# Gate/up units of a fused S4 and feed-forward kernel: a hand-written order of seven slots, and a second DMA queue

## The chip, the cores and the metric

The kernel runs on one core of one Trainium2 chip. The core has a matrix engine (TensorE, PE in the profile), VectorE (DVE), ScalarE (ACT), GpSimd (POOL) and SyncE (SP). Each works through its own instructions in the order in which they were put into its stream, and waits at an instruction until what that instruction needs is there. DMAs are issued from a stream too: here mostly from SP, some from ACT and POOL. The metric is the device time of one execution in microseconds (us), the median of several runs.

## What is computed

`x` is 2048 rows of 1024 floats. Each row is normalized; the result goes through a long convolution along the 1024 columns, whose kernel comes from a small state-space model (S4), and through a feed-forward block with 4-bit weights (64 weights share a scale and a zero). Both are added to `x`:

```python
xn = _layernorm(x, axis=-1)
# S4: 64 states -> 1024 frequencies -> kernel K of 1024 taps
y = jnp.fft.irfft(jnp.fft.rfft(u, n=n) * jnp.fft.rfft(K, n=n), n=n)[..., :L]
return y + D[0] * u
# feed-forward, inter = 2752
g = jnp.einsum('bsh,ih->bsi', x, Wg)
u = jnp.einsum('bsh,ih->bsi', x, Wu)
h = jax.nn.silu(g) * u
return jnp.einsum('bsi,hi->bsh', h, Wd)
```

## The kernel before

**Number format.** Operands of the matmuls are split into two fp16 halves, a high and a low one. A product then takes three matmuls (high·high, high·low, low·high): `PASS`. Every split is a copy to fp16 on ACT (a "hi" step) and a subtraction on DVE (a "lo" step).

**Seven products in place of eight.** The large matrix products use the Strassen-Winograd scheme: of a 2 by 2 product seven block products are made, of sums and differences of blocks. The scheme needs seven factors of each operand (`PROD` names which meet).

**Stages.** First come the norm of `x` and the first weights (to about 135 us). Then the gate/up stage makes `h`; then the convolution (from about 878 us) and the product of `h` with the down weights (from about 1004 us) fill the rest. The change is in the gate/up stage.

**A unit.** The 2752 columns of gate and up are cut into pieces `j` of 128, and the 2048 rows into two halves `cp`. `gate_up(j, cp, wf)` (L597) is one unit: seven products P1 to P7, each 4 x 3 = 12 matmuls of 128x512, into four PSUM banks A, B, C and D. Units for `j` = 0 and 1 are made in another way; `j` = 2 to 20 gives 38 units. P1 goes to A and is copied to B by ACT; P6 adds to B, which is copied to D; P7 goes to C and is copied to the tile `hb`; P2 adds to A. P5 adds to D, and DVE adds D to `hb`; P3 then adds to D; P4 adds to C, which is copied to `ha`, to which DVE adds B. Silu of A and of D on ACT, and two DVE multiplications, give `ha` and `hb`, the two halves of `h`. P5, P4 and P3 of a unit are left for the following unit (`pending`, `rest`, L595 to L612).

**Factors of h.** `finish_h` (L673) makes the factors that the down product will need (`s0` to `s6`) and writes them to DRAM (`HF`), 256 KB each, from SP.

**Weight work beside the units.** It has three kinds. (1) `load_w(gi)` (L409) makes half of the gate/up weights of a piece, a "granule": raw 4-bit values and scales are fetched (`load_raw`), unpacked on DVE, the scales prepared by three instructions on POOL (`scale_c`), sixteen 128x64 activations on ACT apply them (`w_scale`, in three parts), four DVE sums make the factors (`w_sums`), then hi and lo into two tiles `nat`, and two DMA transposes from SP bring them into the tile `wf` that the matmuls read (`w_t`). Four `wf` tiles are there, two pieces' worth. (2) `load_wd(u)` (L461), for u = 0 to 9, makes the factors of the down weights. Its scales and zeros come from DRAM (`SZT`) by four DMAs from SP for each half, in `fetch_wd` (L472); then `dequant`, `sums`, and seven hi and lo steps follow, and each factor goes to DRAM from SP. (3) `s4()` (L853) makes the convolution's kernel by some small DVE operations and a few small matmuls, which borrow a PSUM bank. Both (2) and (3) are generators that the loop of L995 moves on by some steps behind each unit; `lag` (L453) makes a generator wait until a given number of units have ended.

**What sets the order.** In this stage the lines only tell what depends on what. The scheduler of the framework, which runs a model of the times at build, picks the order of the instructions on each engine. Only where an `Engine` has its `pin` set (L66 to L85; at the start of the kernel) does an engine's stream keep the order of the program. Tiles come from pools with a fixed number of buffers: the hi and lo tiles `nat` from five, `ha`/`hb` and their sums from four for even and four for odd `j`, A and C (and S4's banks) from four banks, B and D from two each.

```python
995  for j in range(2, NJ):
996      if 3 <= j < NJ - 1:
997          load_w(2 * j + 2, (j - 1, 1))
998          load_w(2 * j + 3, (j - 1, 1))
999      for cp in range(2):
1000         if cp or j > 3:
1001             gate_up(j, cp, wt[j])
1002         for _ in range(4 if j >= WD_FROM else 0):
1003             next(wd_steps, 0)
1004         for _ in range(3 - cp if j >= S4_FROM else 0):
1005             next(s4_steps, 0)
```

Of the kernel before, what the change touches and what calls it, by code (L numbers as in the profile page):

```python
# [24 lines left out]
F16 = mybir.dt.float16  # L25
# [8 lines left out]
P = 128  # L34
# [4 lines left out]
NJ = 21  # L39
# [48 lines left out]
def build(nc, tc, x, xp, raw_d, sz_d, par_d, vct_d, tab_d, csrow_d, out):  # L88
# [3 lines left out]
    with es:  # L92
# [195 lines left out]
        with ea:  # L288
# [95 lines left out]
            def w_scale(gi, part, behind=None):  # L384
                with tc.issue_after(heads[behind].ins) if behind in heads else nullcontext():
                    scale_a(*made[gi], range((0, 5, 11)[part], (5, 11, 16)[part]))
# [66 lines left out]
            def lag(n=1):  # L453

                n += len(tails)
                while len(tails) < n:
                    yield

            rawd, ready_wd = {}, {}

            def load_wd(u):  # L461
# [10 lines left out]
                def fetch_wd(gi):  # L472


                    raw = rawd.pop(gi)
                    w = wtemp("wd", [P, 8, 256], F32, f"w{gi}")
                    for i in range(2):
                        for b in range(2):
                            SP.dma_start(w[64 * b : 64 * b + 64, 4 * i : 4 * i + 4].rearrange("p f c -> p (f c)"),
                                         SZT[gi - G_WD, 1 - i, b].rearrange("c h -> (c h)").partition_broadcast(64))  # L480
                    q = wtemp("raw", [P, 16, 2, 32], I16, f"qn{gi}")
                    low = raw.bitcast(I16).rearrange("p a (b c) -> p a b c", c=2)[:, :, :, 0]
                    V.tensor_scalar(q[:, :, 0, :], low, 4, 15, ALU.logical_shift_right, ALU.bitwise_and)
                    V.tensor_scalar(q[:, :, 1, :], low, 15, None, ALU.bitwise_and)
                    qt = raw.bitcast(I16).rearrange("p a b -> p (a b)").rearrange("p (a b) -> p a b", a=8)
                    SP.dma_start_transpose(qt, q.rearrange("p a b c -> p (a b c)"))
                    return w, qt

                def dequant(w, qt):
                    x4 = w[:, 0:4]  # L490
                    tt(x4, qt.rearrange("p (f a) b -> p f (a b)", f=4), x4, sub)
                    tt(x4, x4, w[:, 4:8], ALU.mult)
# [16 lines left out]
                if u == 0:  # L509
                    load(ga)  # L510
                    load(gb)
                    yield from lag()
                    ready_wd[ga] = fetch_wd(ga)
                    yield
                ready_wd[gb] = fetch_wd(gb)
                yield from lag(2 if u == 0 else 1)
                ma = ready_wd.pop(ga)
                with tc.issue_after(tails[-1].ins):
                    dequant(*ma)
# [5 lines left out]
                if nxt:  # L525
                    load(nxt[0])
# [4 lines left out]
                lo(5, wa[:, :, 0])  # L531
                mb = ready_wd.pop(gb)
                dequant(*mb)
                wb = blocks(mb[0][:, 0:7])
                yield
                sums(mb[0], True)
                hi(3, wb[:, :, 1])
                tt(wa[:, :, 1], wb[:, :, 1], wa[:, :, 1], sub)
                yield
                if nxt:  # L540
                    load(nxt[1])
                lo(3, wb[:, :, 1])
                hi(7, wa[:, :, 1])
                tt(wb[:, :, 1], wb[:, :, 1], wa[:, :, 0], sub)
                yield

                lo(7, wa[:, :, 1])
                hi(6, wb[:, :, 1])
                if nxt:
                    ready_wd[nxt[0]] = fetch_wd(nxt[0])  # L550
                yield
                hi(2, wb[:, :, 0])
                lo(6, wb[:, :, 1])
# [5 lines left out]
                lo(4, wb[:, :, 0])  # L559
                yield  # L560
# [34 lines left out]
            pending = []  # L595

            def gate_up(j, cp, wf):  # L597
# [12 lines left out]
                def rest(i):  # L610
                    if len(pending) > i:
                        pending[i]()  # L612

                nm = f"{j}_{cp}"
                isc = 1.0 / (XS * WS)
                add, mult = ALU.add, ALU.mult
                bA, bB = bank("A" + nm), bank("B" + nm, "B")
                prod(1, bA, True, True)
                heads[j, cp] = A.copy(bB, bA)
                rest(0)  # L620
                bC = bank("C" + nm)
                prod(7, bC, True, True)
                tag = "h" if j % 2 else "e"
                hb = htile("hb_" + nm, tag)
                A.copy(hb, bC)
                rest(1)
                prod(6, bB, False, True)
                bD = bank("D" + nm, "D")
                A.copy(bD, bB)
                prod(2, bA, False, True)  # L630
                A.activation(bA, bA, AF.Silu, scale=isc)
                rest(2)

                def fifth():
                    prod(5, bD, False, True)
                    tails.append(V.tensor_tensor(hb, bD, hb, add))

                def fourth():
                    prod(4, bC, False, True)
                    ha = htile("ha_" + nm, tag)  # L640
                    A.copy(ha, bC)
                    V.tensor_tensor(ha, bB, ha, add)
                    V.scalar_tensor_tensor(ha, ha, HS * isc, bA, mult, mult)
                    pending[2] = lambda: third(ha)

                def third(ha):
                    prod(3, bD, False, True)
                    A.activation(bD, bD, AF.Silu, scale=isc)
                    V.scalar_tensor_tensor(hb, hb, HS * isc, bD, mult, mult)
                    finish_h(j, cp, ha, hb)  # L650

                pending[:] = [fifth, fourth, None]

            def settle():
                for i in range(len(pending)):
                    pending[i]()
                pending.clear()
# [15 lines left out]
            def finish_h(j, cp, ha, hb):  # L673
                nm = f"{j}_{cp}"
                if j == NJ - 1:
                    for c, h in enumerate((ha, hb)):
                        pc = wtemp("nat", [P, 2, 512], F16, f"hpl{nm}_{c}")
                        split(pc, h)
                        A.dma_start(HPL[cp][:, c, 0:2, :], pc)
                    return  # L680
                def emit(f, src):
                    SP.dma_start(HF[cp][f, :, j // 2, :], src)

                if j % 2 == 0:
                    emit(0, ha)
                    slots[cp] = (ha, hb)
                    return
                s0, s2 = slots.pop(cp)
                s1, s3 = ha, hb
                s4, s6 = (htile(f"s{n}_{nm}") for n in (4, 6))  # L690
                emit(1, s1)
                emit(3, s3)
                V.tensor_tensor(s4, s0, s2, ALU.subtract)
                emit(4, s4)
                V.tensor_tensor(s2, s2, s3, ALU.add)
                emit(2, s2)
                V.tensor_tensor(s0, s2, s0, ALU.subtract)
                emit(5, s0)
                V.tensor_tensor(s6, s1, s0, ALU.subtract)
                emit(6, s6)  # L700
# [8 lines left out]
            def s4_coefficients():  # L709
# [3 lines left out]
                yield from lag(2)  # L713
# [11 lines left out]
                yield  # L725
# [7 lines left out]
                for a in range(2):  # L733
# [4 lines left out]
                    V.scalar_tensor_tensor(cf[:, 4 + 2 * a : 6 + 2 * a], wx[:, 2:4], ur, tmp, ALU.mult, ALU.subtract)  # L738

            def s4_cauchy(qt):  # L740
# [6 lines left out]
                yield  # L747
# [12 lines left out]
                yield from lag(2)  # L760
# [6 lines left out]
                yield  # L767
                V.tensor_copy(s4p[rows, 48:112], ps[rows, 0:64])
                yield

            def s4_kernel():
                tab, tab2, z = (wtemp("nat", [P, 512], F32, f"s4t{i}") for i in range(3))
                tab2 = tab2[:, 0:272]
                SP.dma_start(tab, tab_d[0])
                SP.dma_start(tab2[0:8], tab_d[1, 0:8, 0:272])
# [43 lines left out]
                yield from lag()  # L819
                py = bank("s4y")  # L820
                pk = py[0:8, 256:384]
# [4 lines left out]
                yield  # L826
# [9 lines left out]
                yield from lag()  # L836
# [3 lines left out]
                yield  # L840
# [152 lines left out]
            gate_up(2, 0, wt[2])  # L993
            gate_up(3, 0, wt[3])
            for j in range(2, NJ):  # L995
                if 3 <= j < NJ - 1:
                    load_w(2 * j + 2, (j - 1, 1))
                    load_w(2 * j + 3, (j - 1, 1))
                for cp in range(2):
                    if cp or j > 3:  # L1000
                        gate_up(j, cp, wt[j])
                    for _ in range(4 if j >= WD_FROM else 0):
                        next(wd_steps, 0)
                    for _ in range(3 - cp if j >= S4_FROM else 0):
                        next(s4_steps, 0)
                if j == NJ - 2:
                    for i in range(2):
                        w_unpack(G_WP + i)
                        for part in range(3):
                            w_scale(G_WP + i, part)  # L1010
                        wp_hi(i)
                        wp_lo(i)
            settle()
            for steps in (wd_steps, s4_steps):
                for _ in steps:
                    pass
# [392 lines left out]
```

## Time and profile before

| | us |
|---|---|
| median of 3 runs | 1330.53 |
| lowest and highest | 1329.95 and 1332.14 |
| the profiled execution, its own time | 1331.74 |
| its span, first to last instruction | 1330.0 |

The profile is of one execution. Its span is what the engines' records cover; 1.74 us of that execution's time lie around it. The stages, by the view of busy time in given stretches (a record of a matmul ends after the next has begun, so that PE counts as busy until the end of the last one):

| stretch (us from the start) | length | PE busy | DVE busy | ACT busy | POOL busy | DMA share |
|---|---|---|---|---|---|---|
| 0 to 134.8, norm, first weights, `j` = 0 and 1 | 134.8 | 118.9 | 106.7 | 88.7 | 32.1 | 0.65 |
| 876 to 1004, convolution | 128.0 | 127.4 | 72.5 | 12.6 | 0.0 | 0.62 |
| 1004 to 1330, down product | 326.0 | 321.0 | 255.3 | 117.8 | 98.4 | 0.83 |

The stretch between, 134.8 to 876, is the gate/up stage. In the views below, "L77" is the line of the `Engine` helper and stands for nearly every instruction, so groups are told apart by their tiles: `A`, `B`, `C`, `D` are the banks, `w` the weights being unpacked, `nat` and `nd` the halves of gate/up and of down weights. "x12" counts merged instructions, and a bracket tells how long the engine sat idle before the first of them and what ended that.

### The profile page before, as it was taken

The page shows a single profiled execution, that of the slowest core. Times are in us where ns is not written, and L with a number is a line of the kernel's source. Part 1 is how long each engine was busy: PE and PEld are TensorE (multiplying, and loading weights), DVE is VectorE, ACT ScalarE, POOL GpSimd, SP SyncE. Part 2 cuts the span into 40 slices and gives each one's busy share as a digit, 9 for nine tenths or more (in the row PEclk, how much of TensorE's full clock was granted, in tenths as well). Part 3 has the DMA queues.
Part 4 walks back from the last instruction along what each step waited for, and adds up shares of the span by engine and source line. Part 5 has one row for each costly group of instructions (what it writes and reads, how often), then busy time and mean ns, then how long its engine had stood idle before and what let it go on. Part 6 is the DMA issues. An engine that isn't in the chain of part 4 may idle for free. (4 is left out here: it accounts for less than half of the span.)

```text
span 1330.0 us, 20904 instructions
## 1 busy us (share of the span) xinstructions
PE 1274.0 (96%) x7880; PEld 751.9 (57%) x7880; DVE 987.9 (74%) x1344; ACT 669.2 (50%) x1208; POOL 182.8 (14%) x267
## 2 busy tenths in 40 slices
PE   5999899999999899989989998999999999999998
PEld 5644344444444344444444443456558888888887
DVE  6779967486886877786878777462738898779792
ACT  4867566656656474766568475420204433443330
POOL 3230001010100000000111000000000032256440
PEclk8999899999999999999999998999999999999999
DMA  6791958469887988888798887765837779799981
GB/s 225 173 218 31 196 152 186 97 163 251 212 229 159 240 217 207 223 210 232 191 264 224 216 215 180 216 213 187 333 122 292 273 202 265 238 262 274 285 181 48
DMA packets 358401, 276.04 MB, mean 208 GB/s; under 512 B 211668, under 2 KB 304668, under 8 KB 354204
## 3 DMA queue, kind: packets, MB, share of 16 engines
q1 hardware_dynamic: 335676, 261.59, 70.6%
q0 software_dynamic: 21760, 10.49, 6.6%
q10 hardware_dynamic: 864, 2.62, 0.5%
q8 instruction: 62, 1.02, 0.3%
q14 instruction: 39, 0.32, 0.1%
HBM read 132.36 MB, written 94.84 MB: 171 GB/s over the span
## 5 line engine op out<-in xcount | busy, mean ns | idle before, releaser
L77 PEld LDWEIGHTS <-wf 128*128 128x128 f16 x3960 | 375.7, 99 | 467.8 <-issue 45.2
L77 PEld LDWEIGHTS <-g 128*128 128x128 f16 x2940 | 287.6, 98 | 33.5 <-issue 0.2
L77 ACT ACTIVATE w<-w,sz 128x64 f32<-128x64 int32 x640 | 217.9, 427 | 74.9 <-DVE w L77 58.3
L77 PE MATMUL A<-x,wf 128*128 128x512 f16 x912 | 215.2, 385 | 13.4 <-ACT ha L77 5.3
L77 PE MATMUL D<-x,wf 128*128 128x512 f16 x912 | 211.5, 380 | 14.1 <-DVE hb L77 12.1
L77 PE MATMUL C<-x,wf 128*128 128x512 f16 x912 | 208.0, 381 | 2.8 <-DVE ha L77 2.6
L77 ACT CAST g<-a 128x2560 f16<-128x2560 f32 x42 | 97.5, 2324 | 182.1 <-PE cv L77 52.6
L77 PE MATMUL A<-b,g 128*128 128x256 f16 x1680 | 185.9, 273 | 0.0
L77 DVE TENSOR_TENSOR w<-w 128x256 f32<-128x256 f32 (+2 forms) x272 | 136.9, 527 | 61.2 <-ACT w L77 54.7
L77 DVE TENSOR_TENSOR g<-a,g 128x2560 f16<-128x2560 f32 x42 | 118.4, 2821 | 30.9 <-ACT g L77 30.9
L1261 POOL DMA_DIRECT2D out<-o x64 | 78.8, 2139 | 360.7 <-DVE o L77 348.2
L322 POOL TENSOR_SCALAR sz<-sz 128x16 f32<-128x16 f32 x42 | 18.6, 443 | 673.2 <-DMA sz<-in_sz 622.7
L77 PE MATMUL B<-x,wf 128*128 128x512 f16 x456 | 106.7, 384 | 1.8 <-ACT B L77 1.8
L77 ACT CAST nat<-w 128x896 f16<-128x896 f32 x76 | 68.3, 935 | 72.9 <-issue 34.4
L77 ACT CAST nd<-w 128x896 f16<-128x896 f32 x70 | 64.1, 933 | 68.9 <-DVE w L77 47.6
L77 DVE TENSOR_TENSOR nat<-w,nat 128x896 f16<-128x896 f32 x76 | 81.0, 1087 | 19.3 <-ACT nat L77 19.1
L77 PE MATMUL D<-b,g 128*128 128x256 f16 x840 | 94.0, 273 | 0.0
L77 DVE TENSOR_TENSOR nd<-w,nd 128x896 f16<-128x896 f32 x70 | 75.5, 1086 | 16.3 <-ACT nd L77 16.0
L77 PEld LDWEIGHTS <-x 128*128 128x128 f16 x576 | 52.4, 98 | 23.7 <-issue 2.7
L77 DVE SCALAR_TENSOR_TENSOR p<-cv,p 128x512 f32<-128x512 f32 x32 | 21.9, 688 | 50.3 <-PE cv L77 44.9
L77 PE MATMUL cv<-band,x 128*128 128x512 f16 (+3 forms) x384 | 57.1, 299 | 0.0
L77 PE MATMUL g<-x,wf 128*128 128x128 f16 (+1 forms) x336 | 48.8, 293 | 1.7 <-ACT wf L82 0.8
(145 smaller groups left out, 1203.8 us busy)
## 6 DMA issues: line engine op xcount, KB each, us to landing
a<-HF SPq DMA_DIRECT2D x28, 1280.0 KB, 8.1
WD<-nd SPq DMA_DIRECT2D x70, 448.0 KB, 4.4
b<-WD SPq DMA_DIRECT2D x49, 640.0 KB, 5.9
w<-SZT SPq DMA_DIRECT2D x80, 256.0 KB, 5.7
raw<-in_raw SPq DMA_DIRECT2D x65, 256.0 KB, 3.8
HF<-ha SPq DMA_DIRECT2D x54, 256.0 KB, 2.9
HF<-s SPq DMA_DIRECT2D x40, 256.0 KB, 3.0
HF<-hb SPq DMA_DIRECT2D x36, 256.0 KB, 3.6
```

The lines of the kernel that those rows point to most:

```text
L77: return method(*args, **kw)
L322: G.tensor_scalar(sz[:, 0], sz[:, 0], WS, None, ALU.mult)
L1261: G.dma_start(dst, o[:, q], accum_op=ALU.add)
```

## The change

Five things change.

1. `gate_up` becomes a generator of seven slots, one for each product of its unit or the one before: P1, P5, P7, P4, P6, P3, P2, where P5, P4 and P3 are those of the unit before. The copies, silus, DVE steps and writes of a unit each get a fixed slot, in that unit or one of the two after it (`late`, `queued`). P3 moves ahead of P2.
2. In the loop, PE, ACT, DVE and SP keep the program's order from unit (4, 0) on; for PE the unit (4, 0) itself is left free. POOL is not pinned.
3. The granules from 11 on are cut into steps of one slot each (`granule`), one begun in slot 4 of each unit; the sixteen activations are issued as 4, 6 and 6. Raw values are fetched one granule ahead. Steps of down weights come in slots 2, 4 and 6 (and 0 once S4 is done), S4's in slot 5 and some of slot 0. `lag` goes; S4's last matmuls get a bank of their own.
4. Fetches of the down weights' scales and zeros are issued from POOL in place of SP, and each comes two or more steps ahead of its use.
5. Writes of the factors of `h` are issued from POOL too, for all `j`. The factor `s4` is made with the even piece and not with the odd one.

```diff
-                    scale_a(*made[gi], range((0, 5, 11)[part], (5, 11, 16)[part]))
+                    scale_a(*made[gi], range((0, 4, 10)[part], (4, 10, 16)[part]))
...
-                            SP.dma_start(w[64 * b : 64 * b + 64, 4 * i : 4 * i + 4].rearrange("p f c -> p (f c)"),
+                            G.dma_start(w[64 * b : 64 * b + 64, 4 * i : 4 * i + 4].rearrange("p f c -> p (f c)"),
...
-                with tc.issue_after(tails[-1].ins):
-                    dequant(*ma)
+                dequant(*ma)
+                if nxt:
+                    load(nxt[0])
...
+                lo(6, wb[:, :, 1])
+                hi(2, wb[:, :, 0])
                 if nxt:
                     ready_wd[nxt[0]] = fetch_wd(nxt[0])
...
                 lo(4, wb[:, :, 0])
+                if nxt:
+                    ready_wd[nxt[1]] = fetch_wd(nxt[1])
                 yield
...
                 prod(1, bA, True, True)
+                queued("silu A", "last h")
+                yield
+                queued("P5", "sums")
                 heads[j, cp] = A.copy(bB, bA)
-                rest(0)
+                yield
                 bC = bank("C" + nm)
                 prod(7, bC, True, True)
+                queued("add D")
+                yield
+                queued("P4")
+                yield
+                prod(6, bB, False, True)
+                queued("copy C")
+                yield
+                queued("P3")
+                bD = bank("D" + nm, "D")
+                A.copy(bD, bB)
                 hb = htile("hb_" + nm, tag)
                 A.copy(hb, bC)
+                queued("first h")
+                yield
                 prod(2, bA, False, True)
+                queued("silu D")
...
+            def emit(cp, j, f, src):
+                G.dma_start(HF[cp][f, :, j // 2, :], src)
...
+            def granule(gi):
+                last_i = gi >= G_WP
+                if not gi % 2:
+                    yield
+                w_unpack(gi)
+                w_scale(gi, 0)
+                yield
+                if gi + 1 in ahead:
+                    rawt[gi + 1] = load_raw(gi + 1)
+                w_scale(gi, 1)
+                yield
+                w_scale(gi, 2)
+                yield
+                if not last_i:
+                    w_sums(gi)
+                yield
+                wp_hi(gi - G_WP) if last_i else w_hi(gi)
+                yield
+                wp_lo(gi - G_WP) if last_i else w_lo(gi)
+                yield
+                if not last_i and gi % 2:
+                    w_t(gi)
+                yield
+                yield
+                if not last_i and not gi % 2:
+                    w_t(gi)
+                yield
...
+            for eng in (V, A, SP):
+                eng.pin = True
+            for j in range(4, NJ):
                 for cp in range(2):
+                    PE.pin = (j, cp) != (4, 0)
+                    for n, _ in enumerate(gate_up(j, cp, wt[j])):
+                        if n == 4 and queue:
+                            if queue[0] == G_WP:
+                                rawt[G_WP] = load_raw(G_WP)
+                            under_way.append(granule(queue.pop(0)))
+                        if n in (2, 4, 6) or n == 0 and waits is None:
+                            next(wd_steps, 0)
+                        if waits == "read" or n == 5 or n == 0 and cp and waits != "bank":
+                            waits = s4_next()
+                        for g in list(under_way):
+                            if next(g, 0) == 0:
+                                under_way.remove(g)
             settle()
```

## The prediction

> **What bounds the kernel now.** I read the busy times first, then the stretches, the half-clock stretches inside the gate/up stage, and the waits there.
>
> ```profile
> PE 1274.0 (96%) x7880; PEld 751.9 (57%) x7880; DVE 987.9 (74%) x1344; ACT 669.2 (50%) x1208; POOL 182.8 (14%) x267
> ...
> 134.80:876.00 741.20, 706.79 (x3258) 317.80 (x3259) 553.42 (x914) 450.14 (x975) 52.25 (x108) 0.99 0.81 203
> ```
>
> TensorE is the bound: 96% busy. The stretch row (length, busy PE, PEld, DVE, ACT, POOL, granted clock, DMA share, GB/s) says where it isn't: 741.20 - 706.79 = 34.4 us idle in the gate/up stage. The stages after it have 0.6 and 5.0 us of such idle time.
>
> ```profile
> 138.70:145.50 6.80, 5.87 (x14) 1.92 (x15) 6.80 (x10) 5.13 (x12) 0.00 (x0) 0.50 1.09 167
> 340.10:343.50 3.40, 3.40 (x10) 1.20 (x9) 3.32 (x7) 3.40 (x6) 0.65 (x1) 0.50 1.10 217
> 620.00:623.40 3.40, 3.40 (x10) 1.16 (x9) 2.35 (x6) 1.69 (x3) 0.86 (x3) 0.50 0.97 178
> 804.30:811.10 6.80, 5.51 (x14) 1.92 (x14) 6.80 (x12) 0.00 (x0) 1.57 (x3) 0.50 0.14 30
> 686.60:694.00 7.40, 3.99 (x20) 1.86 (x19) 7.40 (x13) 1.61 (x4) 0.57 (x1) 1.00 0.82 234
> ```
>
> In the first four rows the granted clock is 0.50. PE was busy there for 5.87 + 3.40 + 3.40 + 5.51 = 18.2 us, of which half, 9.1, is lost. Idle and slow time together: 43.5 us. Check from the other side: in the chain of waits twelve matmuls of a product take 2.59 us undisturbed, so 38 units need 38 x 7 x 2.59 = 688.9; the stage, from 134.8 to the convolution's first matmul at 878.25, lasts 743.4. The difference is 54.5; 43.5 of it are explained, and 11.0 are S4's small matmuls (16 took 1.16 us) and what isn't recorded.
>
> Who makes PE wait is seen best at the longest stall:
>
> ```profile
> 794.96 5.41 ACT L77 ACTIVATE w<-w,sz 128x64 f32<-128x64 int32 x16 [1.40 <-DVE w L77]
> ...
> 796.76 3.17 SPq L77 DMA_DIRECT2D w<-SZT  x4
> ...
> 803.71 1.23 DVE L77 TENSOR_TENSOR w<-raw,w 128x1024 f32<-128x1024 int16 x1 [8.28 <-DMA w<-SZT]
> 804.86 0.68 DVE L77 TENSOR_TENSOR hb<-D,hb 128x512 f32<-128x512 f32 x1
> ...
> 805.59 1.01 PE L77 MATMUL D<-x,wf 128*128 128x512 f16 x2 [5.46 <-DVE hb L77]
> ```
>
> PE waits for `hb`, a 0.68 us addition; the addition is not slow, it stands in DVE's stream behind a `dequant` of down weights whose factors, issued late by SP, were 8.28 us away. ACT meanwhile does sixteen activations in one piece. The waits view of 205 to 876 us shows that this is the pattern:
>
> ```profile
> ACT w L77 <- DVE w L77: 53.9, 21, 6.1
> DVE w L77 <- ACT w L77: 50.1, 28, 4.8
> ...
> DVE w L77 <- DMA w<-SZT: 32.9, 10, 8.3
> ...
> PE D L77 <- DVE hb L77: 12.1, 4, 5.5
> ```
>
> So no engine but PE is full; PE stops when weight work that waits stands ahead of a unit's short steps.
>
> **What the order gives back.** In the new order P5's result is needed by P3 three products later (7.8 us for "add D"), B's copy by P6 also three later, and between P4, whose result the copy of C takes to free the bank, and the next P1 that needs a bank lie P6, P3 and P2. A unit's short step can thus be one or two slots late at no cost. Of the 43.5 us, the start stays: P1 of unit (2, 0) waits for weights that older code makes (3.4 idle at 134.6 to 141.1, and half of 5.87 slow), and at 212 to 217 the unit left unpinned waits 1.5, behind `load_w` of granules 8 to 10: 7.8 us. **To be had: 43.5 - 7.8 = 35.7 us.**
>
> Does the slow clock leave with the stalls? The Trainium skill ("TensorE: Matmul & The Clock Gate", What's actually happening) says that the clock halves after an idle window of about 3.4 us. The row at 686.60 shows clock 1.00 after a stall of 3.41 us, while stalls of 1.32 (before 339.0) and 3.02 (before 619.4) were followed by 0.50. By the rule only the stall of 5.46 costs clock (2.8 us of the 6.2 outside the start); by the rows all do. I take the rows; between the two lie 3.4 us.
>
> **Can DVE and ACT keep up?** A unit of PE is 7 x 2.59 = 18.13 us. DVE per unit, from the groups: six operations on `ha`, `hb`, `s` at 0.683 = 4.1; a granule 2 x 0.419 + 4 x 0.419 + 2 x 1.087 = 4.7; down weights 4 x 0.418 + 4 x 1.22 + 8 x 0.419 + 7 x 1.086 + 4 x 1.084 = 21.8 for each of ten u, over 34 units 6.4; S4 some 28 us, 0.8. Sum **16.0**, 88%. ACT: six copies and silus at 0.573 = 3.4; a granule 16 x 0.427 + 2 x 0.935 = 8.7; down weights 70 x 0.933 / 34 = 1.9. Sum **14.0**. Laid out by slot, units alternate on ACT between about 16.5 and 11.5 (22 activations in one, 10 in the next), and DVE's heaviest, with S4, have 18 to 19.3 in four of 34. Both fit, DVE barely. Waits added by pinning: behind DVE's wait for activations in slot 0 of every second unit stand "add D" and the lo of the granule. I place it: ACT ends the third part some 2.3 us into that unit; DVE reaches lo's end at 10.4 to 11.6.
>
> **Weights in time.** After lo come two transposes; SP needs 2.0 us to issue one (four in a row took 8.03) and the median landing is 4.6 us: 17 us into the unit. P1 of the next piece reads that half from 18.13 + 9 x 0.216 = 20.1 on. Margin 3 us, 16 times. DVE late by more costs PE the rest. Between 0 (on time) and 2.3 us each (lo as late as its longest wait for ACT in the waits view, 4.8, with some of the margin left) I take 0.3, as the row of this wait is small now (0.8 us in the whole stretch): **5 us**.
>
> **S4's banks.** Seven small matmul groups stand in PE's fixed order; before, two waited 2.5 us. Bounds 0 and 7 x 1.6 = 11; taken as now: **2.5 us**.
>
> **The second queue.** 126 writes of factors of `h` and 80 fetches leave SP: in a unit 5.9 DMAs. Nearest rows for POOL:
>
> ```profile
> 1191.22 1.20 POOL L1261 DMA_DIRECT2D out<-o  x1 [1.17 <-DMA out<-o]
> ...
> w<-SZT SPq DMA_DIRECT2D x80, 256.0 KB, 5.7
> ...
> out<-o POOLq DMA_DIRECT2D x64, 128.0 KB, 10.5
> out<-U POOLq DMA_DIRECT2D x16, 128.0 KB, 6.4
> ```
>
> 5.9 x 1.20 + 1.36 for `scale_c` = 8.4 us of 18.13, so POOL is not full. Landing: at best SP's 5.7, at worst 10.5; those POOL rows accumulate in DRAM, so I take 6.4. Four fetches land 4 x 1.2 + 6.4 = 11.2 us after the first is issued; the `dequant` that waits is three steps on: 18.1 us at three steps a unit, 13.6 at four. Cost nothing; at 10.5 it would be 15.3, late by 1.7 in the four or five u of the last 14 units. Behind that wait stand, on DVE, the lo and "add D" above. A write's buffer (`hb` of the even piece after next) is wanted some 11 us after its DVE step: hidden too. POOL runs `scale_c` in the same stream, 1.36 us that ACT waits for; a granule's scales come a unit ahead, so 0, or a 1.2 us DMA each where it queues behind one. A rule of the skill speaks against this part: "SBUF — State Buffer" (Summary: rules for kernel authors) says that descriptors of POOL's DMAs starve while DVE runs in its fast modes, and to issue from SP or ACT. Of DVE's work here only the unpacking is of that kind (0.42 us each, 120 of them, 50 us of 741). If every DMA met one, POOL would need 5.9 x 0.42 = 2.5 us more, 10.9 of 18.13. By row or by rule the path is the same.
>
> For `j` = 0, 1 ten `h` writes and four sums leave SP too, before the first transposes; those stood behind writes of `mpc` that don't move. 0, from -2 to +2. The end: P3's last result still passes silu, multiplication, split, DRAM and back (before, 878.25 to 887.99 against 9.1 us of convolution in front): unchanged within 0.5.
>
> **Sum.** -35.7 + 5 + 2.5 = -28.2 us: 1331.74 for the profiled execution becomes 1303.5; its 1.2 above the median goes off too: **1302 us**.
>
> **Rivals.**
> (a) Half of it. Fixed order puts its own waits where the old ones were: the `nat` pool's five tiles (ACT waits 14.1 us for `WD<-nd` writes now), or lo late by 1 us more at each of 16 pieces. 1330.5 - 14 to 21: about **1313**. For it: a fixed stream can't use another product while one waits, as PE did at 207 to 217. Against: slack of two slots.
> (b) DVE becomes the bound: slower. In order DVE has 34 x 18.13 = 616 us for 541 us of work; it may wait 75 us in all, 2.2 us a unit, before PE is slowed, and 3.3 a unit (75 + 35.7) before all is lost. Now it idles 671.0 - 497.28 = 174 us in the 37 units' time of 205 to 876, 4.7 a unit. If it keeps its waits of over 1 us (some 147 us), the stretch lasts 688 and not 666: **1352**. For it: the number itself. Against: 50 us of it wait for sixteen activations that now come a slot ahead, 33 for `SZT`.
> (c) No change: the lost time is elsewhere. Against: every stall above is inside the stage that is rewritten.
>
> **Chances.** Forecast (1291 to 1308) 0.50, (a) 1308 to 1327 0.24, within 0.2% (what a measurement of this kernel can tell from no change) 0.04, (b) 0.22. Faster 0.74. The range reaches from all of the loss regained, 1289, into (b) at 1345, where some 0.13 are left out above and 0.03 below; the likeliest case's own is 1291 to 1308.
>
> **To look for after.** Right: the stage near 713 us, PE idle there below 17, no half clock after 150 us; no wait of PE for `hb`; DVE's wait for `w<-SZT` under 10 us, POOL near 8 us a unit. Wrong: waits of P1 for `wf<-nat` at every piece (then lo is late), DVE over 90% of the stage with PE waiting for it (b), or waits of ACT for `HF` writes or `nat`.

## The result, and the profile after

| | before | after |
|---|---|---|
| median, us | 1331.34 | 1391.53 |
| lowest and highest, us | 1329.95 and 1332.91 | 1375.55 and 1399.33 |
| profiled execution, its span, us | 1330.0 | 1389.1 |

The ratio is 1.0412, with an interval of 1.0324 to 1.05; it compares the means of the fast runs and leaves out the slow one at 1399.33 us, so that it is lower than the ratio of the medians. The changed kernel is 4% slower; 1302 us were forecast, and 1391.53 lies above the range too.

First the busy row of the page of after (busy us, share of the span, instructions), then the gate/up stage in the view of stretches (columns as before), and one stretch of it:

```profile
PE 1283.5 (92%) x7880; PEld 752.2 (54%) x7880; DVE 1008.4 (73%) x1344; ACT 673.4 (48%) x1208; POOL 288.8 (21%) x487
...
134.80:937.62 802.82, 718.12 (x3264) 319.27 (x3263) 574.67 (x919) 452.44 (x973) 156.88 (x323) 0.94 0.84 186
666.50:685.50 19.00, 1.68 (x5) 0.28 (x3) 0.00 (x0) 2.29 (x7) 1.25 (x3) 0.60 1.26 140
```

No engine but POOL is fuller than before, and POOL is busy for 21%. The stage, up to the convolution's first matmul at 937.62, takes 802.82 us where before, counted the same way, took 743.45. Of the 59.4 us more, 50.3 are idle time of TensorE (802.82 - 718.12 = 84.7 against 34.4) and 9.1 are matmuls that ran slower (mean clock 0.94). In the last row PE, DVE, ACT and POOL all but stand still, while the DMA engines count as more than full (1.26; the records overlap) and move only 140 GB/s, against 186 on the average of the stage.

The waits of PE from 205 to 960 us (us in total, times, longest):

```profile
PE A L82 <- DMA wf<-nat: 65.3, 12, 11.5
PE s4s L82 <- ACT ha L82: 10.4, 2, 10.1
PE D L82 <- ACT D L82: 2.3, 1, 2.3
```

The waits for `hb` are gone. In their place P1 waits for the weights of its piece: the transposes are late. The 10.1 us of the second row have the same source, since ACT stands there for 11.33 us at a `nat` tile that a late transpose has not yet read. One such stall in the timeline (start, duration, engine, instruction, and in brackets the idle time and what ended it):

```profile
655.68 2.06 POOL L473 DMA_DIRECT2D w<-SZT  x4 [2.06 <-DVE nd L82]
656.45 14.50 SPq L82 DMA_TRANSPOSE wf<-nat  x2
...
662.67 4.05 PE L82 MATMUL A<-x,wf 128*128 128x512 f16 x18
...
665.72 2.04 POOL L473 DMA_DIRECT2D w<-SZT  x4 [4.46 <-DVE nd L82]
...
671.67 10.94 SPq L82 DMA_TRANSPOSE raw<-qn  x1
673.52 1.46 PE L82 MATMUL A<-x,wf 128*128 128x512 f16 x3 [6.79 <-DMA wf<-nat]
...
686.49 1.46 PE L82 MATMUL A<-x,wf 128*128 128x512 f16 x3 [11.51 <-DMA wf<-nat]
687.81 0.76 DVE L82 TENSOR_SCALAR qn<-raw 128x512 int16<-128x512 int16 x2 [22.39 <-DMA raw<-qn]
```

DVE and ACT were on time: the two transposes begin at 656.45, 6 us ahead of P1. But SP needs 14.50 us to issue the two and not 4, and PE goes on with their weights 17 and 30 us after the first was begun. Beside them POOL's fetches, two groups of four, are on their way, and writes of factors of `h`. The instructions of one tile, and then the page's DMA issues (count, KB each, median us to landing), say the same of the whole kernel:

```profile
L82 SPq DMA_TRANSPOSE wf<-nat x62: 1524/2665/15645, 233.8 to 885.9; - x62
```

```profile
w<-SZT POOLq DMA_DIRECT2D x80, 256.0 KB, 6.9
...
wf<-nat SPq DMA_TRANSPOSE x76, 5.0
...
raw<-qn SPq DMA_TRANSPOSE x20, 10.5
```

Issuing a transpose takes at most 15645 ns (3708 before). The median landing has hardly moved, 5.0 against 4.6: it is the late ones, up to 26.5 us in the stage where before had 6.4 at most, that stop PE.

### The profile page after: what moved, and what is told of

It reads as the page before. It is cut to its first block, busy times and chain, and to the rows that moved or that the text cites. A ratio compares the mean times of both kernels' runs of the same rounds, so it can differ in the third digit from the quotient of the medians.

```text
span 1389.1 us, 20979 instructions
## 1 busy us (share of the span) xinstructions
PE 1283.5 (92%) x7880; PEld 752.2 (54%) x7880; DVE 1008.4 (73%) x1344; ACT 673.4 (48%) x1208; POOL 288.8 (21%) x487
## 4 chain that ended last, share of the span: by engine, by line
PE 47%; DMA 7%; DVE 1%; ACT 1%; issue 0%; SPq 0%; POOL 0%; ACTq 0%; DVEq 0%; POOLq 0%
PE A L77 13%; PE cv L77 7%; PE D L77 7%; DMA wf<-nat 6%; PE D L82 5%; PE C L82 5%; PE A L82 4%; PE E L77 3%; PE B L82 2%; PE cc L77 1%; DMA raw<-qn 1%; DMA hpl<-HPL 0%; ACT w L82 0%; SPq L82 0%; DVE ha L82 0%
## 5 line engine op out<-in xcount | busy, mean ns | idle before, releaser
L82 PE MATMUL A<-x,wf 128*128 128x512 f16 x791 | 188.2, 393 | 66.5 <-DMA wf<-nat 65.3
L82 ACT ACTIVATE w<-w,sz 128x64 f32<-128x64 int32 x560 | 196.0, 428 | 59.4 <-DVE w L82 42.7
L82 PE MATMUL D<-x,wf 128*128 128x512 f16 x816 | 195.9, 392 | 2.3 <-ACT D L82 2.3
L82 PE MATMUL C<-x,wf 128*128 128x512 f16 x804 | 179.4, 379 | 0.0
L82 DVE TENSOR_TENSOR w<-w 128x256 f32<-128x256 f32 (+1 forms) x244 | 132.6, 545 | 44.3 <-ACT w L82 37.3
L82 PE MATMUL B<-x,wf 128*128 128x512 f16 x396 | 90.9, 379 | 0.3 <-ACT B L82 0.3
L82 DVE TENSOR_TENSOR nat<-w,nat 128x896 f16<-128x896 f32 x62 | 65.1, 1086 | 25.6 <-ACT nat L82 25.6
L82 ACT CAST nat<-w 128x896 f16<-128x896 f32 x62 | 55.6, 936 | 45.7 <-DMA wf<-nat 17.5
L689 POOL DMA_DIRECT2D HF<-ha x54 | 30.9, 572 | 168.4 <-DVE ha L82 154.5
L473 POOL DMA_DIRECT2D w<-SZT x80 | 41.8, 532 | 78.6 <-DVE nd L82 39.5
```

Of the source, the lines that this page charges most:

```text
L82: self.last = method(*args, **kw)
L473: G.dma_start(w[64 * b : 64 * b + 64, 4 * i : 4 * i + 4].rearrange("p f c -> p (f c)"), SZT[gi - G_WD, 1 - i, b].rearrange("c h -> (c h)") ...
L689: G.dma_start(HF[cp][f, :, j // 2, :], src)
```

## The experiments

Two theories stood against each other. **M** (mixing): the DMAs of a second queue run beside SP's transposes and hold them up; the order is good. **O** (order): the fixed order itself is bad, the second queue harmless. All ratios are to the kernel before, with their intervals; a difference between two kernels is the difference of their ratios, of 1331 us.

### The change taken apart

The order without the second queue:

```diff
# order_alone, against after
-G.dma_start(w[64 * b : 64 * b + 64, ...   (SZT)
+SP.dma_start(w[64 * b : 64 * b + 64, ...
-G.dma_start(HF[cp][f, :, j // 2, :], src)
+SP.dma_start(HF[cp][f, :, j // 2, :], src)
```

> The changed kernel with both moved groups of DMAs, the writes of the factors of h and the fetches of scales and zeros, issued from SP again: the hand-written order alone. Theory M (mixing: packets of POOL's queue and the 256-byte packets of the weight transposes run on the same DMA engines and slow each other, so that weight tiles come late): no landing of a transpose of gate/up weights over 8 us in the stage (26.5 in the changed kernel), PE's waits for these tiles under 10 us in the stage (65), half-clock time in the stage under 20 us (about 100), time 1295 to 1320 us. Theory O (the order itself: the steps of a granule, or SP's stream in program order, are too late whatever the queue): waits for weight tiles stay at 50 us or more, time 1370 to 1400.

Measured: **1315.27 us**, 0.987 (0.9841 to 0.9898). The waits of PE in the stage:

```profile
PE A L82 <- DMA wf<-nat: 12.6, 9, 3.7
PE D L82 <- ACT D L82: 2.6, 1, 2.6
```

The order alone is 17 us faster than before: O falls. From 220 us to the end of the stage PE, DVE and ACT run the same instructions in the same order in both traces, so it is the queue that costs 72 us (1.0412 - 0.987; the intervals leave some 12 us either way). Two signs of M were missed by a little: the waits are 12.6 us and not under 10, and the slowest transpose landed after 8.3 us and not within 8.

One group of DMAs at a time, the other back on SP:

```diff
# writes_pool: fetches of SZT back on SP, writes of HF on POOL
# fetches_pool: writes of HF back on SP, fetches of SZT on POOL
```

> The changed kernel with the fetches of scales and zeros back on SP; only the writes of the factors of h come from POOL. Theory M: the writes are 140 of the 220 moved DMAs, and every one can meet a transpose, so a part of the loss stays: 1320 to 1370 us, with some transposes landing after 10 us or more. If the writes are harmless and the fetches, four in a row, are what hurts, 1295 to 1320. Theory O: 1370 to 1400.

> The changed kernel with the writes of the factors of h back on SP; only the fetches of scales and zeros come from POOL. Theory M: each fetch is four DMAs of 256 KB and is issued just beside a transpose of the raw down weights, 20 times: 1320 to 1370 us; the transposes of raw down weights stay slow (median landing about 10 us, 10.5 in the changed kernel, 3.6 before). If only the writes hurt, 1295 to 1320 with that median near 4. Theory O: 1370 to 1400.

Measured: writes on POOL **1329.26**, 0.9969 (0.9957 to 0.998); fetches on POOL **1358.53**, 1.0197 (1.0161 to 1.0234). From order_alone on, the writes cost 13 us, the fetches 44, and both together 72. That is 15 more than the sum, which is hardly clear of the noise. PE's waits for `wf`, of writes_pool and of fetches_pool:

```profile
PE A L82 <- DMA wf<-nat: 17.8, 9, 5.9
```

```profile
PE A L82 <- DMA wf<-nat: 40.3, 13, 8.3
```

The queue without the order:

```diff
# queue_alone, against before: both groups issued by G in place of SP
```

> The kernel before with only the two groups of DMAs moved from SP to POOL, in the scheduler's old order. Theory M: the transposes are slowed here too; 1345 to 1390 us, transposes landing after 10 us or more, PE waiting for weight tiles 15 us or more in the stage (0.8 before). Theory O: the queue does nothing, 1325 to 1335.

Measured: **1355.85**, 1.0182 (1.0147 to 1.0216). The queue hurts under the scheduler's order too, by 24 us. It is not quite the old order: nothing is pinned here, and the scheduler moved some instructions (of DVE's 1344, 1180 still stand in the order of before, of PE's 7880, 7671), so the 24 us hold the queue and these moves together. The waits for `wf` are only 8.2 us and not the 15 expected; those for `hb` and for copies of B have grown. That the late DMAs reach PE by way of these other steps was not followed up.

```profile
PE D L77 <- DVE hb L77: 15.4, 4, 5.0
PE B L77 <- ACT B L77: 8.6, 5, 4.5
PE A L77 <- DMA wf<-nat: 8.2, 2, 8.0
```

### POOL's way of issuing, or any second queue

The fetches from ACT's queue, which like SP's is served by hardware:

```diff
# fetches_act, against order_alone
-SP.dma_start(w[64 * b : 64 * b + 64, ...
+A.dma_start(w[64 * b : 64 * b + 64, ...
```

> The hand-written order with writes on SP and the fetches of scales and zeros from ACT's hardware queue, a second queue that is not POOL's. If any second queue beside the transposes hurts: as with the fetches on POOL (1358.5), 1340 to 1370, with landings of transposes over 10 us and the median for raw down weights near 7. If it is POOL's kind of queue alone: 1310 to 1325, like the order alone (1315.3), a few us more where ACT waits at an issue.

Measured: **1387.92**, 1.0429 (1.0384 to 1.0473), worse than from POOL. PE's waits for `wf`:

```profile
PE A L82 <- DMA wf<-nat: 59.6, 16, 12.4
```

So POOL's way of issuing is not needed for the harm: ACT's queue does it too. That it does more harm there is in part another matter, since ACT must issue these fetches between its own steps, and waits at them:

```profile
449.51 13.90 ACTq L82 DMA_DIRECT2D w<-SZT  x3
463.46 2.09 ACT L82 ACTIVATE w<-w,sz 128x64 f32<-128x64 int32 x6 [15.82 <-issue]
```

### The disputed cost by itself

The next three kernels do none of the kernel's computation; they issue DMAs in phases (the code below is shortened): T is twelve transposes of 128x1792 fp16 from SP, and beside them come 24 plain DMAs of 256 KB from POOL (G), ACT (A) or SP itself (S).

```diff
+for phase in ("T", "G", "TG", "A", "TA", "S", "TS", "T", "TG", "TA"):   # mix_measured: writes to DRAM
+for phase in ("T", "fG", "TfG", "fA", "TfA", "fS", "TfS", "C", ...):      # fetch_measured: SZT-like fetches
+for phase in ("T", "fG", "TfG", "fA", "TfA", "fS", "TfS", "T", ...):      # fetch_fenced: the same, phases apart
+    fence()
+    for i in range(12):
+        if "T" in phase: SP.dma_start_transpose(dst[i], src)
+        if second queue in phase: two plain DMAs
```

> Not the kernel's computation at all: phases of plain DMAs, each begun when the one before has landed. In a phase with T, twelve transposes like those of a weight tile (128x1792 fp16, 1792 packets of 256 bytes each) go out from SP; with G, twenty-four writes of 256 KB like those of a factor of h from POOL; with A the same writes from ACT's hardware queue; with S from SP itself, two behind each transpose. Phases in order: T, G, TG, A, TA, S, TS, T, TG, TA. From the rates in the changed kernel (undisturbed 700 to 1100 transpose packets a us, and some 330 KB a us of POOL's packets alone): T alone 20 to 30 us, G alone 17 to 22 us. Theory M in the strong form (the two kinds spoil each other's rate): TG lasts well over the sum of both, 65 to 120 us, while TS, where one queue keeps them apart, stays within 20% of the sum of T and S. If two queues only share the engines, TG is at most the sum of T and G, some 45 us, with the transposes done late in it. If any second queue does it, TA is like TG; if only POOL's, TA stays at the sum or below.

Measured: T 28.7 us, G 20.5, both 53.8 and then 59.4 (sum of the parts 49.2); from ACT 49.7 and 47.9 (sum 46.8), in turn on SP alone 48.9 (sum 47.3). The expected collapse to 65 to 120 us is a miss: with a second queue of writes a phase takes 2 to 21% over the sum. But with a second queue the transposes always end last.

> Again only plain DMAs in phases, each begun when the one before has landed, none of the kernel's computation. T: twelve transposes of 128x1792 from SP. f: twenty-four fetches like those of scales and zeros (a row of 4 KB from DRAM into each of 64 partitions, 256 KB), from POOL (G), ACT (A) or SP (S, two behind each transpose). C: twelve plain copies in SBUF of the same bytes in pieces of 256 bytes, from SP. Phases: T, fG, TfG, fA, TfA, fS, TfS, C, CfG, T, TfG, TfA. With writes in place of fetches the phase of both lasted 54 to 59 us for a sum of 49 (two runs of it in one execution). In the four kernels transposes ran at 176 to 227 packets a us beside fetches, 434 beside writes alone, and some 800 alone. If fetches are what spoils the rate: TfG and TfA last 1.4 times the sum of their parts or more, TfS stays within 1.15. If a fetch and a write are alike and the kernel's slow stretches come from something else there: TfG 1.1 to 1.2 times the sum. If a transpose is what can't stand company: CfG at or below its sum; if any stream of small packets can't: CfG like TfG.

This one is inconclusive. Its fences did not keep later transposes behind earlier fetches, so that phases ran into each other and no sum can be read. I made it again with a chain of DVE steps between phases:

> None of the kernel's computation is done. Phases that do not overlap: T is 12 transposes of 128x1792 fp16 on SP, f is 24 fetches of a 4-KB row into 64 partitions each (from POOL G, ACT A or SP S), Tf both at once; the order is T fG TfG fA TfA fS TfS T TfG TfA TfG TfA. From the stretches of the run before that do not overlap: T alone 26 to 29 us, f alone some 26 us, and beside a full POOL queue 64 transpose packets and 64 packets of 4 KB each us, one for one. Sharing only: TfG and TfA end after the sum of the parts within 10% (52 to 60 us), the fetches first (after some 30 us, having slowed little) and the transposes last, and TfS is the same sum. Loss: TfG or TfA take more than 20% over the sum (over 65 us) while TfS does not.

The starts of that chain's step in DVE's timeline are the ends of phases, here from T to TfA:

```profile
16.29 0.18 DVE L27 CAST src<-st 128x16 f16<-128x16 f32 x1
...
44.94 0.17 DVE L27 CAST src<-st 128x16 f16<-128x16 f32 x1 [26.82 <-DMA dst<-src]
...
74.60 0.17 DVE L27 CAST src<-st 128x16 f16<-128x16 f32 x1
...
121.49 0.15 DVE L26 COPY st<-w 128x1 f32<-128x1 f32 x1 [2.14 <-DMA w<-in_x]
139.36 0.17 DVE L27 CAST src<-st 128x16 f16<-128x16 f32 x1 [17.72 <-DMA dst<-src]
...
169.14 0.17 DVE L27 CAST src<-st 128x16 f16<-128x16 f32 x1
...
229.45 0.17 DVE L27 CAST src<-st 128x16 f16<-128x16 f32 x1 [15.29 <-DMA dst<-src]
```

T takes 28.7 us, fetches from POOL 29.7, both 64.8: the last fetch has landed after 46.9 us (121.49), and DVE then still waits 17.72 us for transposes. Three such phases took 64.8, 55.8 and 68.1 us (sum of the parts 58.3), three with ACT 60.3, 57.6 and 60.4, and the same DMAs in turn on SP alone 50.5. The total is near "sharing", so the loss of over 20% did not show; but the transposes' part of it is large. Counted from the trace's DMA records:

```
packets started per us           transposes (256 B)   fetches (4 KB, and their 4-B ones)
20 to 40 us, T alone                  828                 -
50 to 70 us, fetches alone             -                  73
180 to 185 us, both, from ACT          71.2               61.6
347 to 369 us, both, from POOL         65.5               65.4
485 to 495 us, both, from POOL        109                 32
```

The fourth row shows one mechanism: **packet for packet**. As many packets of the one kind start as of the other, so each of the 16 engines seems to take one packet from each queue in turn, and a transpose's packet of 256 bytes (28 ns) waits for a fetch's of 4 KB (288 ns). The transposes fall to a thirteenth of their rate, while the fetches lose a tenth. The third row shows nearly the same beside ACT. This is what the Trainium skill states in "DMA: Bandwidth & Descriptors" (Queues, rings and completion order): an engine goes round between queues one packet at a time. The fifth row shows a second state in which both are slow: 109 of 828 and 32 of 73 make 0.57 of what the engines can do, and a transpose's packet takes 121 ns on the mean, where alone it takes 22.

On SP alone the two kinds take turns instead. In the bins of 1 us from 273 us on, 304, 997, 491, 0, 420 and 1018 transpose packets start, and 31, 0, 54, 57, 17 and 0 of 4 KB.

The same count for the kernels, over the bins of 1 us of the stage with transpose packets and at least five 4-KB packets of the second queue. The last column adds each kind's share of the rate that it has alone (828 transpose packets per us, 59 of 4 KB for a fetch and 86 for a write); other packets of SP in these bins are not in it. Bins with transpose packets and nothing else give 0.93 to 0.99.

```
               bins   transposes/us   4-KB packets/us   share of the engines' work
writes_pool      77        367               40               0.91
fetches_pool     87        143               27               0.63
fetches_act     137        196               22               0.60
order_alone       0         -                 -                -
```

In the kernels little is lost beside writes, the engines are shared. Beside fetches of `SZT` over a third of the engines' work is lost as well, from POOL as from ACT. The long stall shown for after lies in this second state: from 666.5 to 685.5 us 143 transpose packets and 25 packets of POOL's queue start per us, 0.17 + 0.35 = 0.52.

What brings the second state on was not found. It is not the fetches as such: in the phases without the kernel the same sum, over all bins with both kinds, is 0.72, 0.95 and 0.68 beside POOL's fetches, but also 0.76 and 0.64 beside POOL's writes. There the second queue has 24 DMAs to work through; in the kernel fetches come four in a row and writes mostly by one or two. No run varied how many are in flight, nor the shape of the fetches (a DRAM row of 4 KB into each of 64 partitions).

### What is left of the order's gain

order_alone still waits 12.6 us for `wf`. Is that SP's own queue? In its timeline of SP the transposes of one granule stand behind four fetches and a transpose that were put in just ahead:

```profile
579.70 3.06 SPq L82 DMA_DIRECT2D w<-SZT  x4
582.86 1.26 SPq L82 DMA_TRANSPOSE raw<-qn  x1
584.22 7.45 SPq L82 DMA_TRANSPOSE wf<-nat  x2
```

First, each slot's granule step ahead of its weight step:

```diff
# granule_first, against order_alone
+                        for g in list(under_way):
+                            if next(g, 0) == 0:
+                                under_way.remove(g)
                         if n in (2, 4, 6) or n == 0 and waits is None:
                             next(wd_steps, 0)
```

> The hand-written order, all moved DMAs back on SP, and in each slot the granule's step is put ahead of the steps of down weights and S4, so that DVE makes the halves of a gate/up tile earlier and SP issues its transposes ahead of the fetches of the same slot. In the order alone PE still waited 12.6 us for such tiles, the longest where four fetches and a transpose stood just ahead on SP. Theory M with the order's own rest (those waits are queueing on SP and DVE): waits for weight tiles under 4 us in the stage, 1298 to 1310. If the rest is not queueing but the transposes' own length: no change, 1312 to 1318.

Measured: **1317.22**, 0.9895 (0.986 to 0.9931), waits for `wf` 12.6 as in order_alone: a miss. A wait of PE for ACT lasts 5.5 us, where order_alone had 2.6:

```profile
PE D L82 <- ACT D L82: 5.5, 1, 5.5
```

The edit left the odd granule's transposes in slot 3, behind the fetches of slot 2, where the timeline of SP finds them again:

```profile
575.75 2.81 SPq L82 DMA_DIRECT2D w<-SZT  x4
578.65 1.26 SPq L82 DMA_TRANSPOSE raw<-qn  x1
580.02 7.40 SPq L82 DMA_TRANSPOSE wf<-nat  x2
```

Then the transposes into the slot of their lo, one earlier, and the last granules' raw values and scales a granule ahead:

```diff
# tile_early, against granule_first
+                nx = G_WP if gi == 2 * NJ - 1 else gi + 1
-                if gi + 1 in ahead:
-                    rawt[gi + 1] = load_raw(gi + 1)
+                if nx in ahead:
+                    rawt[nx] = load_raw(nx)
...
                 wp_lo(gi - G_WP) if last_i else w_lo(gi)
-                yield
                 if not last_i and gi % 2:
                     w_t(gi)
                 yield
+                yield
...
-                            if queue[0] == G_WP:
-                                rawt[G_WP] = load_raw(G_WP)
```

> The hand-written order on SP alone, granule first in each slot, and two more edits: the transposes of an odd granule are issued in the slot of its lo step, not one slot on, so that they stand ahead of the four fetches and the transpose of raw down weights of the same slot; and the raw values of the last two granules are fetched a granule ahead, as the others are (PE waited 5.5 us for them in the run with the granule first). If the rest of PE's waits is queueing on SP: waits for weight tiles under 5 us in the stage (12.6 without these edits) and none of over 2 us for ACT near the end, 1300 to 1310. If not: 1312 to 1318.

Measured: **1297.5**, 0.9739 (0.972 to 0.9758), the fastest of all and faster than both kernels. Its waits of PE, and its stage:

```profile
PE A L82 <- DMA wf<-nat: 2.9, 2, 2.1
```

```profile
134.80:843.72 708.92, 701.15 (x3268) 317.36 (x3269) 576.81 (x921) 454.16 (x976) 47.44 (x112) 0.99 0.86 212
```

The stage lasts 708.92 us and PE idles 7.8: some 5 of it are waits of the first units, which the change leaves alone, and the rest the waits shown. (The 7.8 us that the prediction left standing are another sum, 4.9 of idle time and 2.9 of slow clock; that the figures agree is chance.) The waits for `wf` have shrunk by 9.7 us against granule_first and the wait for ACT of 5.5 is gone. The two edits were made together, so what each is worth was not measured.

## Why the prediction was wrong

**The step that failed** is "The second queue": "By row or by rule the path is the same", at a cost of nothing. It looked for the price on POOL, in its stream and its descriptors, and in the landing of the DMAs that move. The price was paid by DMAs that do not move: the transposes on SP. "Weights in time" took their landing, 4.6 us, from a trace in which, in this stage, nearly every packet ran through SP's queue, and set 3 us of margin against it; in after it is 5.6 us at the median and 26.5 at most. With packet for packet, one group of four fetches (256 packets of 4 KB and 64 small ones) takes 320 / 65.4 = 4.9 us, in which a transpose gets 320 packets in place of some 4000: late by 4.5 us, over the margin, and two groups and the writes can fall together. That is an estimate from the counts above, of sharing alone; the longest stalls, with 0.52 of the engines' work done, are more than sharing. What was measured is 72 us between order_alone and after; how they divide into sharing and loss was not, and the cause of the loss stays open. The range did not hold because no bound of the sum was a slowed transpose.

The other points:

- **The order gives back 35.7 us**: nearly right. Together with "weights in time" and S4's banks the sum was -28.2; order_alone gave -17, with 12.6 us of waits for `wf` where 5 were taken: more than the term. With all on SP again, fetches stand ahead of transposes there, which the prediction, with the fetches on POOL, had no reason to count. With the transposes put ahead, tile_early gives -35; but that is a different kernel from the one forecast, and its 1297.5 does not make the 1302 right.
- **DVE and ACT keep up**: right. DVE has some 575 us of work in the stage (574.67 in after, 576.81 in tile_early), and in tile_early it is done in 708.92. Rival (b) named the right side (slower) for the wrong reason: in the long stall of after, from 666.5 to 685.5 us, DVE did nothing.
- **POOL is not full**: right. Four fetches took POOL 2.06 us, 0.5 each and not 1.20, and `SZT` landed in 6.9 us, near the 6.4 taken. The rule of the Trainium skill that the prediction names ("SBUF — State Buffer", Summary: rules for kernel authors) offers ACT or SP in place of POOL. SP was better, ACT was not (1387.92 us). Starved descriptors are thus not needed for the loss; whether they have a part in it was not tested (a fetch's issue took POOL 0.51 to 0.66 us in after).
- **S4's banks, 2.5 us**: small, as said; in order_alone PE waits 0.3 us for them.
- **The clock**: the rows held against the rule of 3.4 us. In tile_early the longest wait of PE in the stage is 2.11 us, up to 689.58; three matmuls and a wait of 0.76 us follow, and then a stretch at half clock:

```profile
691.60:695.00 3.40, 3.40 (x10) 1.28 (x9) 2.94 (x4) 3.40 (x11) 0.00 (x0) 0.52 0.98 281
```

- **To look for**: "waits of P1 for `wf<-nat` at every piece" was named as the sign of a wrong forecast, and it came (12 waits); but the reason set beside it, that lo is late, was not the reason.

## What to carry to other kernels

Before DMAs are moved to a second queue, ask what they ran behind and what they will run beside: within one queue a transfer with small packets had the engines nearly to itself while its turn lasted, and with a second queue, where that was full, a large packet came between every two of its small ones. Look for the transfers with the smallest packets and the least margin, not only at those that move. And where a change has two parts that can be undone by themselves, run each alone: here one part was worth -17 us and the other +72.

## What the runs showed of the hardware

- Two queues share a DMA engine packet for packet: 65.5 packets of 256 B and 65.4 of the fetches per us, where alone they run at 828 and 73 (fetch_fenced).
- Beside a second queue the engines can also lose work outright: in the kernel over a third beside fetches (0.63 and 0.60), little beside writes (0.91), and in the phases without the kernel about a third at the most beside either (0.68 and 0.64). The reason is open.
- A transpose's issue occupied SP for up to 15.6 us in after, against 5.0 at most in order_alone, and what stands behind it in SP's stream waits as well: `raw<-qn` landed after 10.5 us at the median, against 6.0 in order_alone (3.6 before, in the scheduler's order).
- From ACT's queue the fetches did more harm (+74 us over order_alone) than from POOL's (+44). ACT's own waits at these issues, up to 15.82 us, are in that, so the two queues are not compared by it.
